# Renewing differences of keys at the changes of heads and of images, in a fused attention and non-local kernel

## The chip, the cores and the metric

The kernel runs on one core of a Trainium2 chip. The metric is the device time of one execution in microseconds (us); several executions are timed, and their median is given. One more execution is recorded by the hardware profiler; its page and its trace are what is read here. The engines are called PE (TensorE; PEld is its loading of weights), DVE (VectorE), ACT (ScalarE), POOL (GpSimd) and SP (SyncE, which here only issues transfers).

## What is computed

The input x is two images of 256 channels and 64 x 64 points, in float32. Layer 0 is full attention over the N = 4096 points of an image, with 8 heads of 32 channels, then a projection and a residual. Layer 1 is a non-local block (a second, smaller attention against pooled keys, with a normalization folded in), which follows it for each image. The part that the change touches belongs to layer 0:

```python
qkv = jnp.einsum('oc,bchw->bohw', w_qkv, x)
q, k, v = jnp.split(qkv, 3, axis=1)
...
scores = jnp.einsum('bhdi,bhdj->bhij', q, k) / jnp.sqrt(jnp.asarray(d, x.dtype))
attn = jax.nn.softmax(scores, axis=-1)
out = jnp.einsum('bhij,bhdj->bhdi', attn, v)
out = out.reshape(b, c, h, w)
return jnp.einsum('oc,bchw->bohw', w_proj, out) + x
```

## The kernel before

**Groups, blocks, steps.** The 8 heads of an image are worked in two groups of four, so that four heads of 32 channels fill 128 partitions. With two images there are four groups, n = 0 to 3 (the list QUAD, line 167, of pairs of image b and group qd). A group has 8 blocks of 512 queries (i = 0 to 7, NI = 8), and a block has 32 steps of 128 keys (j = 0 to 31, NJ = 32); this is the triple loop from line 576. Going from n = 0 to 1 and from 2 to 3 is a *change of heads* (the same image, the other four heads); going from 1 to 2 is the *change of images*: between the two groups stand the projection (project, line 629) and layer 1 (non_local, line 653) of the first image, and then the second image begins.

**A step.** PE makes scores of 128 keys against 512 queries of four heads, into two tiles of PSUM (score, line 439). ACT takes exp of each (line 598). PE weighs the values of the step before with their probabilities (weigh, line 472, its matmuls are line 476), and DVE or ACT takes the result from PSUM. The scores of a block stay in the same two tiles of PSUM from step to step: in place of writing new scores, a step *adds* to the old ones the product of the queries with the *difference* between its keys and those of the step before. The steps go through the keys in the order that line 437 gives: one 128-key part of each of the 8 chunks of 512 keys, then the next part of each. The differences lie in four tiles:

- kd (two differences, chunk 1 minus 0 and 3 minus 2), made anew for each group
- last_kd (two: 5 minus 4 and 7 minus 6), one tile for the whole program, line 223
- mid_kd (three: 2 minus 1, 4 minus 3, 6 minus 5), one tile, line 231
- turn_kd (from the last chunk's part to the next part of chunk 0), one tile, line 232

Within a block, score reads mid_kd at steps with j mod 8 = 2, 4, 6, last_kd at 5 (its first half) and 7 (its second half), and turn_kd at 8, 16 and 24.

**Maxima run ahead.** The softmax needs the greatest score of each query before its exponentials. These are worked out by a second pass over queries and keys, roughly one block ahead, in between the steps (maxima, line 382; product, line 290, with its matmuls at line 293). For two heads of four it uses differences too (pair, line 307): kd, and then last_kd. The maxima of a new group's first block run while the old group's last block still needs the old last_kd. For them before_all (line 275) makes the new group's two differences once more, in a tile first_kd, by two subtractions on POOL (line 227). The tile first_kd is a buffer of the pool xs under the tag "x", which has only one buffer: the loads of x for new queries, keys and values (make, line 171), first_kd, and the projection's weights (late_weights, line 97) take turns in it.

**Renewal.** renew (line 245) is called at the even steps: in blocks i > 0 while there is a next group, and in block 0 of groups 1 to 3. In a group's last block it makes the next group's mid_kd by POOL at steps 26, 28 and 30, when the last step that reads each third is over (between, line 234). In the next group's block 0, at steps 0 and 2, ACT copies the two halves of first_kd into last_kd (line 257), and at step 2 POOL makes turn_kd (rounds, line 238).

**Sums and buffers.** The sums of probabilities are made on two ways. Those of heads 0 and 1 are added by POOL at each step (line 509; the last one of a block is line 518). Those of heads 2 and 3 are kept for pairs of steps in tiles of 1024 KB (tag "two", five buffers) and added by accumulating transfers that POOL issues (line 515). When a block is over, normalize (line 520) adds the two accumulators by one more such transfer (line 524) and POOL adds the halves ("whole", line 528); then PE sums over the keys (line 536), ACT takes the result (line 544), the reciprocal goes by way of DRAM (lines 553 to 562, SP's queue), and POOL scales the block (line 573). For the last block of an image line 536 takes the sums as they are and DVE makes the reciprocal (line 547), in the midst of project. The tag "one" has six buffers for the probabilities of heads 0 and 1; project puts the loads x_res (line 635) into them.

**What sets the order.** [...]A scheduler lays the order down from the program's text, the dependences and its own costs: an operation may be placed earlier on its engine than the text has it. tc.issue_after only says that on that engine an instruction stands behind another; it is no wait. Waits on other engines and on buffers are put in by the framework.

Of the kernel before, what the change touches and what calls it, by code (L numbers as in the profile page):

```python
# [19 lines left out]
QUADS = HEADS // QH  # L20
# [5 lines left out]
NI = N // NB  # L26
NJ = N // P
# [8 lines left out]
def conv_attention(  # L36
# [13 lines left out]
    nc = tc.nc  # L50
# [17 lines left out]
    def scores(name):  # L68
        return ps_s.tile([P, 2, NB], F32, tag="s", name=name)
# [6 lines left out]
    def single(name):  # L76
        return probs.tile([P, 2, NB], F32, tag="one", name=name, bufs=ONES)

    def double(name):
        return probs.tile([P, 2, 2, NB], F32, tag="two", name=name, bufs=TWOS)  # L80
# [86 lines left out]
    QUAD = [(b, qd) for b in range(B) for qd in range(QUADS)]  # L167
# [55 lines left out]
    last_kd = const.tile([P, NI // 4, NB], F32, name="last_kd")  # L223

    def differences(n, c, to):
        two = k[n][:, bass.ts(c, 2 * NB)]
        nc.gpsimd.tensor_sub(to, two[:, NB:], two[:, :NB])
# [6 lines left out]
    def between(n, c):  # L234
        two = k[n][:, NB * (2 * c + 1) : NB * (2 * c + 3)]
        nc.gpsimd.tensor_sub(mid_kd[:, c, :], two[:, NB:], two[:, :NB])

    def rounds(n):
        nc.gpsimd.tensor_sub(
            turn_kd,  # L240
            k[n][:, P:NB].rearrange("p (a n) -> p a n", n=P),
            k[n][:, N - NB : N - P].rearrange("p (a n) -> p a n", n=P),
        )

    def renew(i, j, n):


        if (i, j) == (NI - 1, NJ - 6):
            between(n + 1, 0)
        elif (i, j) == (NI - 1, NJ - 4):  # L250
            between(n + 1, 1)
        elif (i, j) == (NI - 1, NJ - 2):
            between(n + 1, 2)
        elif (i, j) == (0, 2):
            rounds(n)
        if i == 0 and j in (0, 2):
            nc.scalar.copy(last_kd[:, j // 2, :], first_kd[n][:, j // 2, :])

# [1 line left out]
    first_kd = {}  # L262
# [159 lines left out]
    def attend(b, y):  # L422
# [73 lines left out]
        added = None  # L496
# [79 lines left out]
        for qd in range(QUADS):  # L576
            for i in range(NI):
                blk = Block(qd, i)
                items = during(blk.n, i)
                both = [None, None]  # L580
                for j in range(NJ):
                    if j % 2 == 0:
                        two = double(f"p_{blk.name}_{j}_1")
                    p = [single(f"p_{blk.name}_{j}_0"), two[:, j % 2]]
                    for pair in (1, 0):
                        if j == 0:
                            s = both[pair] = scores(f"s_{blk.name}_{j}_{pair}")
                            subtract(s, pair, blk)
                            advance(maxes)
                            score(s, pair, blk, j)  # L590
                        else:
                            s = both[pair]
                            score(s, pair, blk, j)
                            advance(maxes)
                        with ExitStack() as order:
                            if cut is not None:
                                order.enter_context(tc.issue_after(cut.ins))
                            nc.scalar.activation(p[pair], s, AF.Exp, scale=scale)  # L598
                    if waiting is not None:
                        weigh(*waiting)  # L600
                        if j == 0:
                            normal = normalize(waiting[0])
                    add(blk, j, p, two)
                    waiting = blk, j, p
                    if j in (1, 5) or j >= AFTER:
                        advance(normal)
                    if j % 2 == 0:
                        make_rows()
                        if i > 0 and blk.n + 1 < len(QUAD) or i == 0 and blk.n > 0:
                            with tc.issue_after(added.ins) if added else ExitStack():  # L610
                                renew(i, j, blk.n)
                        if i == NI // 2 and j in (12, 14) and blk.n + 1 < len(QUAD):
                            if j == 12:
                                kd[blk.n + 1] = qkv.tile(
                                    [P, NI // 4, NB], F32, tag="kd", name=f"kd_{blk.n + 1}"
                                )
                            with tc.issue_after(added.ins):
                                differences(blk.n + 1, j // 2 - 6, kd[blk.n + 1][:, j // 2 - 6, :])
                        if (i, j) == (NI - 1, 8) and blk.n + 1 < len(QUAD):
                            with tc.issue_after(added.ins):  # L620
                                before_all(blk.n + 1)
                    for item in items.get(j, ()):
                        if item[1] < len(QUAD):
                            advance(make(*item), 9)
# [290 lines left out]
```

## Time and profile before

| | |
|---|---|
| median of 3 executions | 3904.28 us (3903.01, 3904.28, 3907.87) |
| profiled execution, its own time | 3908.37 us |
| its span, first to last instruction | 3906.6 us, 69965 instructions |
| mean granted clock of PE | 0.997 |
| change of heads, n = 0 to 1 | copies at 903.5 and 910.1 us |
| change of images, n = 1 to 2 | copies at 1720.3 and 1726.9; projection's matmuls from 1734.85 |
| change of heads, n = 2 to 3 | copies at 2830.6 and 2837.1 us |

Times within the profile are counted from the span's start. A line of a group of instructions has the source line, the engine, the operation, the tiles (out<-in), shapes and the count; then durations in ns. In a line of the timeline stand the start, the time covered, the engine, the source line, the operation and the count, and in brackets how long the engine stood idle before it and what ended that. In a line of stretches stand the stretch, its length, each engine's busy time with the number of its instructions, PE's granted clock, the share of the transfer engines and GB/s.

The steps can be read off as the distance from the start of one weighing (line 476) to the next. Typical steps take 2.96 us; those in which keys, values or queries are made take more (6.85 us at step 30, 4.87 at 11, for example), and where a block's denominators are summed, 3.82. The last five distances of four blocks, and the first nine of the blocks after a change of heads beside an ordinary one, all in us:

```
end of an ordinary block (n = 1, i = 1)      2.96 2.96 6.85 3.13 2.96
end of an ordinary block (n = 3, i = 1)      2.96 2.96 3.29 3.13 2.96
end before a change of heads (n = 0, i = 7)  2.96 3.28 3.29 3.42 2.96
end before a change of heads (n = 2, i = 7)  2.96 3.28 3.29 3.42 2.96
first steps, ordinary (n = 1, i = 1)         2.96 2.96 2.96 2.96 2.96 2.96 2.96 3.82 2.96
first steps after a change (n = 1, i = 0)    2.96 2.96 2.96 2.96 2.96 4.14 2.96 5.09 2.96
first steps after a change (n = 3, i = 0)    2.96 2.96 2.96 4.74 2.96 5.13 2.96 4.34 2.96
```

### The profile page before, as it was taken

What the parts mean: (1) busy time and instruction counts of PE and PEld (TensorE: products, weight loads), DVE (VectorE), ACT (ScalarE), POOL (GpSimd) and SP (SyncE); (2) the same over time, 40 slices, a digit from 0 to 9 for tenths busy, and PEclk for the clock granted to TensorE, in tenths of its full rate; (3) what the DMA queues carried; (4) which work ended last, traced back from release to release, by engine and by line L of the source; (5) the groups of instructions that cost most, each with busy time, mean ns of one, the idle gap of its engine ahead of it and who ended that gap; (6) DMA issues with size and microseconds to landing.
All of it is one profiled execution on the core that took longest, in us unless ns stands there. A gap on an engine that the chain in (4) does not pass through costs nothing.

```text
span 3906.6 us, 69965 instructions
## 1 busy us (share of the span) xinstructions
PE 3864.0 (99%) x27452; PEld 1366.8 (35%) x27452; DVE 2900.7 (74%) x5449; ACT 2697.5 (69%) x3378; POOL 3091.5 (79%) x1957
## 2 busy tenths in 40 slices
PE   9999999999999999999999999999999999999998
PEld 4333333333333333333333333333333333332333
DVE  5888888788888888764458888888888888884444
ACT  5787777777777777751137777777778888887111
POOL 1888899899989999871448899998999999997043
PEclk9999999999999999999999999999999999999999
DMA  1778878778878788780018888887788888889100
GB/s 57 145 167 169 172 166 170 168 162 172 168 167 169 166 168 169 167 188 6 22 34 169 168 175 168 173 171 164 163 176 171 170 170 170 168 168 188 53 17 27
DMA packets 112300, 566.26 MB, mean 145 GB/s; under 512 B 20200, under 2 KB 22504, under 8 KB 50784
## 3 DMA queue, kind: packets, MB, share of 16 engines
q0 software_dynamic: 68832, 501.25, 63.5%
q1 hardware_dynamic: 42448, 59.74, 4.5%
q8 instruction: 215, 3.52, 0.3%
q14 instruction: 117, 0.96, 0.1%
q10 hardware_dynamic: 688, 0.79, 0.1%
HBM read 51.63 MB, written 8.88 MB: 15 GB/s over the span
## 4 chain that ended last, share of the span: by engine, by line
PE 96%; DVE 2%; DMA 1%; POOL 1%; issue 0%; ACT 0%; DVEq 0%; POOLq 0%; ACTq 0%; SPq 0%
PE s L452 28%; PE w L476 26%; PE ps L293 23%; PE y L771 6%; PE q L197 2%; PE k L197 2%; PE v L185 2%; PE proj L639 1%; PE g L696 1%; DVE r L785 1%; PE f L739 1%; PE f L805 1%; PE den L536 1%; DMA p<-p 1%; PE tp L680 0%; PE tp L676 0%
## 5 line engine op out<-in xcount | busy, mean ns | idle before, releaser
L509 POOL TENSOR_TENSOR p<-p,p 128x1024 f32<-128x1024 f32 x945 | 2364.4, 2502 | 281.4 <-ACT p L598 262.7
L598 ACT ACTIVATE p<-s 128x1024 f32<-128x1024 f32 x2048 | 2087.6, 1023 | 560.5 <-PE ps L293 495.1
L293 PE MATMUL ps<-k,q 32*128 32x512 f32 x6142 | 2020.6, 626 | 2.5 <-DVE r L785 1.3
L305 DVE TENSOR_REDUCE part<-ps 128x1 f32<-128x512 f32 x2046 | 1315.7, 686 | 566.8 <-PE ps L293 563.1
L476 PE MATMUL w<-p,v 128*32 128x512 f32 x8192 | 1091.0, 605 | 1.1 <-ACT p L598 1.1
L452 PE MATMUL s<-q,mid_kd 32*128 32x512 f32 x3072 | 771.2, 615 | 0.0
L320 DVE CUSTOM_DVE_ANT_0 ps<-ps,over 128x512 f32<-128x512 f32 x1025 | 706.2, 691 | 24.9 <-PE ps L293 10.5
L491 DVE TENSOR_TENSOR y<-y,w 128x512 f32<-128x512 f32 x961 | 659.1, 686 | 51.9 <-PE w L476 49.3
L293 PEld LDWEIGHTS ps<-k,q 32*128 32x128 f32 x6142 | 625.1, 183 | 25.6 <-DVE part L320 10.4
L313 ACT ACTIVATE over<-ps 128x512 f32<-128x512 f32 x961 | 569.3, 592 | 10.7 <-PE ps L293 7.9
L293 PE MATMUL ps<-kd,q 32*128 32x512 f32 x1056 | 525.9, 593 | 0.0
L452 PE MATMUL s<-q,last_kd 32*128 32x512 f32 x2048 | 508.5, 615 | 4.5 <-ACT p L598 4.5
L452 PE MATMUL s<-q,kd 32*128 32x512 f32 x2048 | 510.5, 616 | 0.4 <-ACT p L598 0.3
L293 PE MATMUL ps<-last_kd,q 32*128 32x512 f32 x904 | 445.1, 590 | 0.0
L476 PEld LDWEIGHTS w<-p,v 128*32 128x32 f32 x8192 | 161.6, 108 | 805.3 <-DVE part L305 775.2
L452 PEld LDWEIGHTS s<-q,mid_kd 32*128 32x128 f32 x3072 | 270.4, 183 | 443.5 <-ACT over L313 253.9
L515 POOL DMA_DIRECT2D p<-p x448 | 395.3, 882 | 27.3 <-ACT p L598 27.1
L452 PEld LDWEIGHTS s<-q,kd 32*128 32x128 f32 x2048 | 174.0, 184 | 299.8 <-ACT over L313 182.7
L452 PEld LDWEIGHTS s<-q,last_kd 32*128 32x128 f32 x2048 | 172.8, 183 | 284.9 <-ACT over L313 178.5
L771 PE MATMUL y<-p,kv 128*128 128x512 f32 x512 | 240.1, 608 | 6.4 <-DVE r L785 6.4
L820 ACT ACTIVATE p<-f 128x1024 f32<-128x1024 f32 x64 | 65.5, 1023 | 248.5 <-PE f L805 219.2
L767 POOL TENSOR_TENSOR sums<-sums,p 128x512 f32<-128x512 f32 x96 | 121.3, 1264 | 113.7 <-ACT p L820 109.9
(120 smaller groups left out, 2806.3 us busy)
## 6 DMA issues: line engine op xcount, KB each, us to landing
p<-p POOLq DMA_DIRECT2D x478, 1024.0 KB, 7.6
x_q<-in_x_dram SPq DMA_DIRECT2D x30, 512.0 KB
x_k<-in_x_dram SPq DMA_DIRECT2D x24, 512.0 KB
x_res<-in_x_dram SPq DMA_DIRECT2D x16, 512.0 KB
out_dram<-z SPq DMA_DIRECT2D x16, 512.0 KB
r<-flat SPq DMA_DIRECT2D x120, 64.0 KB
x<-in_x_dram SPq DMA_DIRECT2D x8, 512.0 KB
wqk_sb<-in_wqk_dram ACTq DMA_DIRECT2D x1, 512.0 KB
```

The source lines that it names most:

```text
L197: nc.tensor.matmul(pq, wqk_sb[:, c, qd, 0 if what == "q" else 1, :], xc[:, c, :], start=(c == 0), stop=(c == NC - 1),)
L293: nc.tensor.matmul(ps, q[n, i][bass.ts(h, D), bass.ts(g, P)], keys[bass.ts(h, D), :], start=True, stop=True,)
L305: reduced = nc.vector.tensor_reduce(part[:, g, h, j : j + 1], ps, AX.X, ALU.max)
L313: cut = nc.scalar.activation(over, ps, AF.Relu)
L320: reduced = nc.vector.tensor_tensor_reduce(out=ps, in0=ps, in1=over, scale=1.0, scalar=LEAST, op0=ALU.add, op1=ALU.max, accum_out=part[:, ...
L452: nc.tensor.matmul(s[:, t, :], kj[bass.ts(h, D), :], q[blk.n, blk.i][bass.ts(h, D), :], start=False, stop=True, skip_group_check=j > 0,)
L476: nc.tensor.matmul(w[bass.ts(h, D), :], v[blk.n][:, keys(j), h, :], p[h // 2][:, h % 2, :], start=True, stop=True,)
L491: nc.vector.tensor_add(blk.num, blk.num, w)
L509: added = nc.gpsimd.tensor_add(blk.sums[0], blk.sums[0], p[0])
L515: sent = nc.gpsimd.dma_start(out=blk.sums[n], in_=two, accum_op=ALU.add)
L598: nc.scalar.activation(p[pair], s, AF.Exp, scale=scale)
L771: nc.tensor.matmul(acc[i][o], wg[:, 2 * t + j, bass.ts(o, P)], p[:, j, :], **edge)
```

## The change

The function renew is written anew, and its caller calls it at every even step. In words:

- At a change of heads (the next group belongs to the same image) the two copies on ACT go. The first half of last_kd is filled by a transfer that SP issues at step 30 of the old group's last block, the second half by one issued at step 0 of the new group's first block; both read first_kd. The third difference of mid_kd moves from step 30 of the old block to step 0 of the new one. turn_kd moves from step 2 to step 4.
- At the change of images first_kd is no longer copied. All three differences of mid_kd, turn_kd and both halves of last_kd are made by POOL from the new group's keys, and all of them are written at step 0 of the new image's first block. (Before, mid_kd was written in the old image's last block, and last_kd came from first_kd.)

```diff
     def renew(i, j, n):
-        if (i, j) == (NI - 1, NJ - 6):
-            between(n + 1, 0)
-        elif (i, j) == (NI - 1, NJ - 4):
-            between(n + 1, 1)
-        elif (i, j) == (NI - 1, NJ - 2):
-            between(n + 1, 2)
-        elif (i, j) == (0, 2):
+        b, qd = QUAD[n]
+        if i == NI - 1 and qd < QUADS - 1:
+            if j in (NJ - 6, NJ - 4):
+                between(n + 1, (j - NJ + 6) // 2)
+            elif j == NJ - 2:
+                nc.sync.dma_start(out=last_kd[:, 0, :], in_=first_kd[n + 1][:, 0, :])
+        elif i == 0 and j == 0 and n > 0:
+            if qd > 0:
+                nc.sync.dma_start(out=last_kd[:, 1, :], in_=first_kd[n][:, 1, :])
+                between(n, 2)
+            else:
+                for c in range(NI // 2 - 1):
+                    between(n, c)
+                rounds(n)
+                for c in range(2):
+                    differences(n, NI // 4 + c, last_kd[:, c, :])
+        elif (i, j) == (0, 4) and qd > 0:
             rounds(n)
-        if i == 0 and j in (0, 2):
-            nc.scalar.copy(last_kd[:, j // 2, :], first_kd[n][:, j // 2, :])
...
                     if j % 2 == 0:
                         make_rows()
-                        if i > 0 and blk.n + 1 < len(QUAD) or i == 0 and blk.n > 0:
-                            with tc.issue_after(added.ins) if added else ExitStack():
-                                renew(i, j, blk.n)
+                        with tc.issue_after(added.ins) if added else ExitStack():
+                            renew(i, j, blk.n)
```

The built programs differ as follows, engine by engine. PE and DVE execute the same instructions in the same order. ACT loses six copies. SP gains four transfers: both of each change of heads stand behind the transfers of the sixth block's denominators and ahead of the next load of x; at the change of images g's two weights move ahead of the load x_res 6. POOL has two more subtractions. At a change of heads mid_kd's third difference stands behind the old block's last addition (line 518), and turn_kd two additions later than before. At the change of images the scheduler has placed all six subtractions in the old image's last block, between the additions of steps 23 and 31: turn_kd ahead of step 24's, mid_kd ahead of 26's, 28's and 30's, last_kd ahead of 29's and 31's; before, only the three of mid_kd stood there, behind 26's, 28's and 30's.

## The prediction

> **What bounds the kernel now.** I read the busy shares and the chain of waits first, then every instruction that touches the tiles of the change, then the timeline around the three changes of group.
>
> ```profile
> PE 3864.0 (99%) x27452; PEld 1366.8 (35%) x27452; DVE 2900.7 (74%) x5449; ACT 2697.5 (69%) x3378; POOL 3091.5 (79%) x1957
> ...
> PE 96%; DVE 2%; DMA 1%; POOL 1%; issue 0%; ACT 0%; DVEq 0%; POOLq 0%; ACTq 0%; SPq 0%
> ```
>
> TensorE carries 96% of the chain. So only what makes PE wait or run slower counts. In the timeline of line 476 (one weighing for each step of 128 keys) nearly every step takes 2.96 us; a change gains where a step at a change of group is longer than the same step elsewhere.
>
> ```profile
> L257 ACT COPY last_kd<-first_kd x6: 612/613/614, 903.5 to 2837.1; 128x512 f32<-128x512 f32 x6
> ...
> L236 POOL TENSOR_TENSOR mid_kd<-k x12: 1264/1268/1287, 17.3 to 2842.2; 128x512 f32<-128x512 f32 x12
> ...
> L239 POOL TENSOR_TENSOR turn_kd<-k x4: 996/1154/1301, 53.3 to 2856.8; 128x384 f32<-128x384 f32 x4
> ```
>
> These are the operations that the change removes or moves: six copies on ACT of 0.61 us, subtractions on POOL of 1.27 us (512 columns) and some 1.15 us (384). The dear place is the change of images:
>
> ```profile
> 1726.89 0.61 ACT L257 COPY last_kd<-first_kd 128x512 f32<-128x512 f32 x1
> ...
> 1727.57 0.40 SPq L103 DMA_DIRECT2D weights<-in_wproj_dram  x1
> ...
> 1728.97 1.06 PE L476 MATMUL w<-p,v 128*32 128x512 f32 x8 [1.14 <-ACT p L598]
> 1734.85 6.43 PE L639 MATMUL proj<-y,weights 128*128 128x512 f32 x9 [4.81 <-DMA weights<-in_wproj_dram]
> ...
> 1732.00:1740.00 8.00, 5.15 (x7) 2.36 (x8) 0.00 (x0) 0.00 (x0) 5.55 (x4) 0.57 1.01 258
> ```
>
> The projection's weights go into the buffer that first_kd holds, so their load is issued only when the second copy is over (1727.51), and PE stands 4.81 us for it. Then it runs at a granted clock of 0.57 (the last line, 1732 to 1740 us). At the two changes of heads something else waits:
>
> ```profile
> 924.76 0.87 POOL L524 DMA_DIRECT2D p<-p  x1 [2.78 <-DMA p<-p]
> ...
> 931.69 1.02 ACT L598 ACTIVATE p<-s 128x1024 f32<-128x1024 f32 x1 [1.90 <-DMA p<-p]
> ...
> 939.28 1.02 ACT L598 ACTIVATE p<-s 128x1024 f32<-128x1024 f32 x1 [2.38 <-POOL whole L528]
> ...
> 2853.92 0.87 POOL L524 DMA_DIRECT2D p<-p  x1 [4.95 <-DMA p<-p]
> ...
> 2861.55 1.02 ACT L598 ACTIVATE p<-s 128x1024 f32<-128x1024 f32 x1 [2.88 <-DMA p<-p]
> ...
> 2868.39 1.02 ACT L598 ACTIVATE p<-s 128x1024 f32<-128x1024 f32 x1 [1.63 <-POOL whole L528]
> ```
>
> POOL, which has not been idle for over 0.15 us at a time since 842 us, stands before line 524 until the old block's last accumulating transfer (line 515, issued 916.42) has landed; everything behind it is late, and the exponentials find no free buffer. By the steps: 4.14 for 2.96 and 5.09 for 3.82 us (2.45 lost) after the first change of heads; 4.74, 5.13 for 2.96 and 4.34 for 3.82 (4.47 lost) after the second.
>
> **What the skill says.** "TensorE: Matmul & The Clock Gate", What's actually happening: PE falls to half clock after an idle window of some 3.4 us of a free-running grid. The trace agrees: its clock record has half speed for 6.83 us from 1732.71, 2.7 us after the last weighing ended at 1730.03. "DMA: Bandwidth & Descriptors", Issuing engines are not separate DMA queues: all transfers share 16 engines. The trace agrees, and shows more: the load of x issued by SP at 910.74 moved its first packet 4.7 us later, when the accumulation issued at 909.57 was nearly through. The same page, Anatomy of one DMA, gives 2.0 us plus bytes over 436 GB/s: 4.4 us for 1024 KB, where the page of this profile has 7.6, so I don't use it.
>
> **The change, part by part.**
> *Copies off ACT.* The closing steps of a block without K and V to make are 2.96, 2.96, 3.29, 3.13 us (blocks of the last group); before a change of heads they are 2.96, 3.28, 3.29, 3.42. So two copies cost 0.32 + 0.29 = 0.61 us of PE, not 1.23. At the change of images the second stands straight before the last exponential, on which PE waits: 0.32 + 0.61 = 0.9 us. On a change of heads the 0.61 gains nothing by itself: what follows waits for POOL's queue, whose times do not depend on ACT there.
>
> *Change of images.* In the built program's order the weights now wait for PE's last read of first_kd, which in the trace is at 1710.6, not for a copy. Four issues of 0.40 to 1.44 us put them on the rings by about 1716, 14 us before PE wants them. The wait of 4.81 us goes. With it the half clock: the seven starts from 1734.85 to 1740.25 take 5.40 us where full speed takes 7 x 0.43 = 3.0, 2.4 lost. What is late next: "later" holds only for the text of the program. In the built order the scheduler puts all renewals before the old image's last addition: POOL has turn_kd (1.15 us) moved ahead and two subtractions into last_kd (2 x 1.27) added, and it is in arrears there (gaps of 0.08 us). So the last transfer of sums (line 515, 1733.09) is issued 1.15 + 1.27 = 2.4 us later, at 1735.5; the last addition (line 518, over at 1736.34) is over 3.7 us later, at 1740.0; the loads of x_res, which take over buffers that those additions free, are issued from some 1722 to 1740 instead of 1732.3 to 1736.4. PE, starting to project at about 1729.3, needs the denominators after 32 matmuls x 0.43 = 13.8 us, at 1743.1, and the transfer (8.5 to 9 us with two loads beside it; it took 10.0 before) lands at about 1744.3. The first four matmuls need older sums and take about 0.8; I charge 0.4 us. The order of loads of x_res and g's weights in SP's queue also changes; x_res was never late by more than 0.8 us in all, nothing. Sum: 0.9 + 4.8 + 2.4 - 0.4 = **7.7 us**, bounds 4 (half clock stays, sums are late by 1 more) and 8.2.
>
> *Changes of heads.* Two transfers of 256 KB each replace the copies. No row shows an SBUF copy by SP's queue. From above, a quarter of an accumulation of 1024 KB (some 5.2 us of all 16 engines in the packet records): 1.3 us of the rings; from below, half a 512 KB load of x (some 1.6): 0.8. I take 0.8. The first is issued when the last step's scores have been read (903.4, 2830.5), moves between two accumulations and costs nothing; the rings are empty from 908 to 910.5. Its reader comes 7 steps later, 20 us. The second is issued at 909.9 beside the accumulation of 909.57. Behind both in SP's queue stand x's next load (used at step 11, over 30 us on) and the transfers of denominators (first needed at 942): room enough. The third difference (mid_kd) moves behind the last accumulation's issue and the addition of line 518: that transfer is issued 1.27 us earlier. mid_kd is then ready at 919.4, for use at step 6 (929). turn_kd moves behind two additions: ready at some 932.6 instead of 929.0, for step 8 (936.2); 3.6 us of room.
> The landing comes earlier by at most 1.27 us at the first change, minus what the rings lose: x's load of 512 KB lay before that transfer and may still, and 256 KB come on top. Bounds -0.3 and 1.2; I take **0.6**. At the second change the loads of x, gw and ww (1 MB, issued 2837.8 to 2842) pushed that transfer to a landing at 2853.38, 10.0 us after its issue; if the new order keeps them behind it, 3.5 us are to be had, of which they give some back before line 524's transfer; if not, 1. Bounds 0.5 and 3; I take **1.7**. POOL's queue sets all later times up to "whole", so these are the gains of PE.
>
> Sum: 7.7 + 0.6 + 1.7 = 10.0 us. The profiled execution took 3908.37 us, 1.8 over its span of 3906.6: it would take 3898.4. It is 4.1 us above the median of the three runs; part may be a second half-clock stretch at 2022.84 (6.83 us, some 3 lost), which depends on where the grid falls and may come or go. I subtract from the median: 3904.28 - 10.0 = **3894.3 us**. A difference of 0.2% (7.8 us) is about what a measurement of this kernel can tell from no change.
>
> **The rivals.**
> *A, forecast, 0.62:* 3891 to 3896.4.
> *B, the changes of heads are cleared whole, 0.10:* all 2.45 + 4.47 + 2 x 0.61 = 8.1 us there, with 7.7: 3888.5. For it: POOL's gap of 4.95 us at 2853.92 is pure waiting. Against: POOL does the same subtractions before "whole" as before.
> *C, the wait for weights becomes a wait for sums, 0.24:* POOL's 3.7 us more in arrears, and half clock at another place; the change of images gives 4 and the heads 0.5: 3899.8, no change that can be told. For it: POOL's gaps of 0.08 us. Against: denominators stood finished 8 us before use (landed 1743.1, used 1751.1).
> *D, slower, 0.04:* the copies hold the rings ahead of the old block's last accumulations. Each us that such a landing is late passes through line 524 to the exponentials. From 16 us in both changes together it outweighs 7.7 and 8 more: about 3913. It needs a copy of 256 KB to take 8 us instead of 0.8 to 1.3.
> That the renewals between images don't come later is not a rival but counted above.
>
> **How the numbers follow.** Faster by over 0.2%: A and B, 0.72; within: C, 0.24; slower: D, 0.04. The range covers A and C, with B and D (0.14) left out: 3890 to 3901.
>
> **What would show it.** Line 639's first matmul starts within 0.3 us of the last weighing, no half clock near it, weights issued at about 1711 to 1716. Line 536 at the change of images waits under 1 us. Closing steps before a change of heads are 2.96, 2.96, 3.29, 3.13. The landing before line 524 comes 0 to 1.2 and 1 to 3.5 us earlier against POOL's own work. Wrong if PE still stands over 2 us at line 639 or 536, or if exponentials wait longer for line 524 than 1.9 and 2.9 us in sum with the rest.

## The result, and the profile after

| | before | after |
|---|---|---|
| median (22 runs each, taken together) | 3904.86 us | 3899.11 us |
| lowest and highest | 3903.01, 3912.77 | 3896.64, 3906.32 |
| profiled execution: own time, span | 3908.37, 3906.6 | 3898.32, 3896.5 |
| its mean granted clock of PE | 0.997 | 0.999 |

The ratio is 0.9985, with a 95% interval of 0.9978 to 0.9991: 5.8 us less, between 3.5 and 8.6. The forecast was 10.0 less (0.9974). The two profiled executions differ by 10.1 us, but a single execution of this kernel scatters by some us, as will be seen.

In the changed kernel the lines behind renew stand lower: 293 is now 301, 476 is 484, 515 is 523, 518 is 526, 524 is 532, 528 is 536, 536 is 544, 598 is 606, 639 is 646. The page's busy shares and its chain of waits are almost the same; the change is too small for them.

```profile
PE 3859.2 (99%) x27452; PEld 1362.3 (35%) x27452; DVE 2899.8 (74%) x5449; ACT 2694.4 (69%) x3372; POOL 3092.7 (79%) x1959
...
PE 95%; DVE 2%; DMA 1%; POOL 1%; issue 0%; ACT 0%; DVEq 0%; POOLq 0%; ACTq 0%
```

**The change of images.** The timeline of SP's queue, of PE, and the stretch from 1732 to 1740 us, all of the changed kernel:

```profile
1712.27 0.40 SPq L103 DMA_DIRECT2D weights<-in_wproj_dram  x1
```

```profile
1729.07 1.07 PE L484 MATMUL w<-p,v 128*32 128x512 f32 x8 [0.63 <-ACT p L606]
1730.07 14.00 PE L646 MATMUL proj<-y,weights 128*128 128x512 f32 x32
1744.00 1.06 PE L544 MATMUL den<-p,ones 128*32 128x512 f32 x8
1745.67 2.77 PE L544 MATMUL den<-p,ones 128*32 128x512 f32 x12 [0.60 <-DMA p<-p]
```

```profile
1732.00:1740.00 8.00, 8.00 (x20) 3.50 (x19) 2.45 (x2) 0.00 (x0) 8.00 (x7) 1.00 1.00 248
```

The denominators of the kernel before, on PE's timeline:

```profile
1751.08 3.64 PE L536 MATMUL den<-p,ones 128*32 128x512 f32 x20
```

The weights are issued 15 us earlier than before, and the projection starts straight behind the last weighing, with no bracket of idle time. The granted clock of the stretch is 1.00 where it was 0.57. One small wait has come: after eight matmuls of the denominators PE stands 0.60 us until the last transfer of sums has landed.

**The changes of heads.** The two transfers and x's next load in SP's queue at the first change; then POOL's issues of the last accumulation (line 523) and of the adding transfer (line 532), and its addition of the halves, whole (line 536); then ACT's exponentials with their waits at both changes, all of the changed kernel:

```profile
903.01 0.53 SPq L253 DMA_DIRECT2D last_kd<-first_kd  x1
909.27 0.49 SPq L256 DMA_DIRECT2D last_kd<-first_kd  x1
911.62 0.40 SPq L88 DMA_DIRECT2D x_q<-in_x_dram  x1
```

```profile
914.74 0.86 POOL L523 DMA_DIRECT2D p<-p  x1
...
925.42 0.87 POOL L532 DMA_DIRECT2D p<-p  x1 [3.88 <-DMA p<-p]
...
937.38 2.65 POOL L536 TENSOR_TENSOR whole<-p 128x1024 f32<-128x1024 f32 x1
```

```profile
924.97 1.02 ACT L606 ACTIVATE p<-s 128x1024 f32<-128x1024 f32 x1 [2.10 <-DMA p<-p]
...
932.36 1.02 ACT L606 ACTIVATE p<-s 128x1024 f32<-128x1024 f32 x1 [2.19 <-DMA p<-p]
...
940.06 1.03 ACT L606 ACTIVATE p<-s 128x1024 f32<-128x1024 f32 x1 [2.49 <-POOL whole L536]
...
2839.71 1.02 ACT L606 ACTIVATE p<-s 128x1024 f32<-128x1024 f32 x1 [2.38 <-DMA p<-p]
...
2853.28 1.02 ACT L606 ACTIVATE p<-s 128x1024 f32<-128x1024 f32 x1 [2.46 <-PE w L484]
```

In the kernel before, x's next load, the last accumulation and whole stood at the first change so:

```profile
910.74 0.40 SPq L88 DMA_DIRECT2D x_q<-in_x_dram  x1
```

```profile
916.42 0.85 POOL L515 DMA_DIRECT2D p<-p  x1
...
936.61 2.64 POOL L528 TENSOR_TENSOR whole<-p 128x1024 f32<-128x1024 f32 x1
```

At the first change POOL's wait before the adding transfer has grown from 2.78 to 3.88 us, and an exponential now waits 2.10 us for the last accumulation itself, and another 2.19 us for the adding transfer. The waits at both places have changed their form; whether PE gained can only be told from a sum over blocks.

**A measure that reads the changes of heads in one number.** The closing steps, the exponentials and the waits shift time between them, so I sum the old group's last block and the new group's first, from weighing to weighing. In the same count (from the first weighing of the old group's last block) stand below the issue and landing of the old block's last accumulation, the landing of the adding transfer, and the end of whole on POOL. All in us:

| change | kernel | last accumulation | adding transfer lands | whole ends | two blocks |
|---|---|---|---|---|---|
| 0 to 1 | before | 98.85 to 106.64 | 114.03 | 121.67 | 202.87 |
| 0 to 1 | after | 97.61 to 107.75 | 115.15 | 122.90 | 204.10 |
| 2 to 3 | before | 98.74 to 108.72 | 116.81 | 123.70 | 201.34 |
| 2 to 3 | after | 97.48 to 106.91 | 115.62 | 122.04 | 199.68 |

The two blocks take whole's end plus 81.20 us at the first change and plus 77.64 at the second, in both kernels. So one time decides: when whole is over. The first change loses 1.23 us, the second gains 1.66. Over all fourteen traces of this study the same two figures hold to 0.03 us at 21 of the 28 changes of heads; of the other seven, five have a stretch at half clock behind the change, and two are those of the kernel with two renewals left out.

The whole difference of the two profiled executions: change of images 7.2 (388.74 us before and 381.52 after, from the first weighing of the old image's last block to the first matmul of line 301, before it 293, with which the next image begins; then another 0.9, where a half-clock stretch lasted 3.41 us in place of 6.83), changes of heads -1.23 and +1.66, ahead of the first weighing 0.4, from the last block on 1.3, all other blocks -0.2: 10.0 us. Of these, 7.2 - 1.23 + 1.66 = 7.6 us lie where the change touches the program.

### The profile page after: what moved, and what is told of

The parts are those of the page before. It is cut to its first block, busy times and chain, and to the rows that moved or that the text cites. A ratio compares the mean times of both kernels' runs of the same rounds, so it can differ in the third digit from the quotient of the medians.

```text
span 3896.5 us, 69971 instructions
## 1 busy us (share of the span) xinstructions
PE 3859.2 (99%) x27452; PEld 1362.3 (35%) x27452; DVE 2899.8 (74%) x5449; ACT 2694.4 (69%) x3372; POOL 3092.7 (79%) x1959
## 4 chain that ended last, share of the span: by engine, by line
PE 95%; DVE 2%; DMA 1%; POOL 1%; issue 0%; ACT 0%; DVEq 0%; POOLq 0%; ACTq 0%
PE s L460 28%; PE w L484 26%; PE ps L301 23%; PE y L778 6%; PE q L197 2%; PE k L197 2%; PE v L185 2%; PE g L703 1%; DVE r L792 1%; PE f L746 1%; PE f L812 1%; PE proj L646 1%; DMA p<-p 1%; PE den L544 1%; PE tp L687 0%; PE tp L683 0%
```

## The experiments

Theory 1 after the result: the change of images brings all of it, and the changes of heads give and take in about equal parts. Theory 2: the heads bring a good part. Three kernels take one half of the change each or another way to the same end, and one is the kernel before once more. Each is shown as a diff against the changed kernel, unless another is named, or in words; the diffs are shortened, and (i, j) ahead of a colon stands for the condition under which the call is made.

**Images alone.** At the changes of heads, renew as before; at the change of images as changed.

```diff
-elif i == NI - 1 and j == NJ - 2: nc.sync.dma_start(out=last_kd[:, 0, :], ...)
-(0, 0): nc.sync.dma_start(out=last_kd[:, 1, :], ...); between(n, 2)     (0, 4): rounds(n)
+j = NJ - 2: between(n + 1, 2)     (0, 2): rounds(n)
+(0, 0), (0, 2): nc.scalar.copy(last_kd[:, j // 2, :], first_kd[n][:, j // 2, :])
```

> The change of images as in the changed kernel, the two changes of heads as in the kernel before. Theory 1 (the image change earns all, the head changes next to nothing): from the last block of group 1 to the first weighing of group 2 some 387.5 us instead of 395.6, the head changes' blocks as before (98.7 + 104.1 and 98.7 + 102.6 us), time 0.9980 of before. Theory 2 (the head changes earn a good part of the 5.8 us): 0.9990 or more.

Measured: 3900.2 against 3906.58 us, ratio 0.9983 [0.9975, 0.9991]. As much as the whole change gave (0.9985), within the intervals. Two blocks: 202.91 us, as before, and 202.08, with 3.41 us at half clock in it.

**Heads alone.** The other half: the changed text at the changes of heads, the old one at the change of images.

> The two changes of heads as in the changed kernel, the change of images as in the kernel before (copies on ACT, PE's wait for the weights stays). Theory 1: the transfers lengthen the accumulations that are under way; the blocks at the first change of heads take some 204.1 us instead of 202.9, at the second 199.7 instead of 201.3; time 1.0000 of before within 0.0006. Theory 2 (as predicted, 2.3 us earned here, or more): 0.9994 or less, both pairs of blocks shorter.

Measured: 3907.16 against 3906.58 us, ratio 1.0001 [0.9992, 1.0009]. Two blocks: 204.20 and 199.72 us, the changed kernel's own numbers to 0.1. The wait for the weights is back (4.72 us), and the 6.83 us at half clock with it. Theory 2 falls by its two blocks, which had to be shorter at both changes; the interval alone would still hold its 0.9994.

**Another release of the weights.** Heads as before. At the change of images only the two copies of first_kd are replaced; mid_kd and turn_kd stay where they were. (The diff is against the kernel before.)

```diff
-nc.scalar.copy(last_kd[:, j // 2, :], first_kd[n][:, j // 2, :])
+differences(n, NI // 4 + j // 2, last_kd[:, j // 2, :])
```

> As the kernel before, only that at the change of images last_kd is made by POOL from the keys instead of being copied from first_kd, at the places in the text where the copies stood. mid_kd and turn_kd stay. Theory (the freed buffer is the whole gain): weights issued at about 1711 us, no wait at the projection, no half clock there, and the last transfer of sums lands about 1.2 us earlier than in the changed kernel, so PE's wait of 0.6 us ahead of line 536's work goes too: group 1's last block to group 2's first weighing in 387 us or less, time 0.9979. Rival (the renewals' new places in POOL's order are part of the gain): 388.5 or more.

Measured: 3900.82 against 3906.58 us, ratio 0.9980 [0.9973, 0.9988]. Its stretch from the last block's first weighing to the next image's first is 386.25 us (before 395.59, after 387.47), and PE's timeline has no wait in it:

```profile
1727.70 14.00 PE L645 MATMUL proj<-y,weights 128*128 128x512 f32 x32
1741.63 3.64 PE L543 MATMUL den<-p,ones 128*32 128x512 f32 x20
```

The twenty matmuls of the denominators run through. So what pays is that nothing reads first_kd late. Up to the first matmul of the next image this stretch is 0.76 us shorter than the changed kernel's, of which the wait is 0.60: that is what the new places of mid_kd and turn_kd cost. The other 0.46 us lie behind that point, where the changed kernel has 3.41 us at half clock and this one has none.

**The kernel before, again.**

> The kernel before once more, for a second profile and for the scatter of the comparison. Expected 1.0000 within 0.0006. If half clock after the change of images (2022.84 us in the first profile) depends on where a free-running grid falls, its place or length differs here; the half clock at the projection (PE idle 4.8 us) is there again, with 1.5 to 3.4 us lost; the distances at the changes of heads repeat within 0.2 us.

Measured: 3907.39 against 3906.58 us, ratio 1.0001 [0.9993, 1.001]. Its trace shows what scatters: the wait for the weights was 5.63 us in place of 4.81, the half-clock stretch near 2024 us lasted 3.41 in place of 6.83, there was another of 3.41 at 3625, and from the last block on it took 379.0 us in place of 376.2. Profiles of single executions can't settle 2 us of the whole; sums over two blocks can, since they repeat to 0.2 us (202.74 and 201.20 here, 202.87 and 201.34 in the first).

The next four ask what the heads' part is made of. All have the changed kernel's change of images. Theory 1: POOL's new order (third difference of mid_kd behind the last addition) gives the gain, the transfers take it back on the rings (the 16 transfer engines with their queues).

**ACT's copies, POOL's new order.**

```diff
-nc.sync.dma_start(out=last_kd[:, c, :], in_=first_kd[...][:, c, :])     (c = 0 at step 30, c = 1 at step 0)
+nc.scalar.copy(last_kd[:, j // 2, :], first_kd[n][:, j // 2, :])     (at steps 0 and 2)
```

> As the changed kernel at the change of images; at the changes of heads the two copies stay on ACT (at steps 0 and 2, as before), while POOL's order is that of the changed kernel (third of mid_kd behind the old block's last addition, turn_kd two additions later). Sums of the last and the first nine-step stretch, read as whole blocks: before 98.74 and 104.14 us at the first change, 98.73 and 102.61 at the second; changed kernel 98.11, 106.00 and 98.11, 101.57. Theory 1 (POOL's new order gives the gain, the two transfers take it back on the rings): the first block after the change falls to about 103 at the first change and to 101 or less at the second, the last block stays at 98.7; heads give 2 to 4 us in sum, 3896 to 3898 us when before is 3906. Theory 2 (POOL's new order is what costs, since line 518 and turn_kd are late): the first change stays at 106 and the whole is 3901.

Measured: 3900.11 against 3905.84 us, ratio 0.9984 [0.9978, 0.9991]; two blocks 202.60 and 201.68. The last accumulation is issued 1.2 us earlier, at 97.65 and 97.48, but lands only 0.4 earlier at the first change (106.25) and 0.2 later at the second (108.94). The new order alone gives next to nothing: both theories missed, the first most of all.

**Transfers, POOL's old order.**

```diff
-(0, 0): between(n, 2)     (0, 4): rounds(n)
+j = NJ - 2: between(n + 1, 2)     (0, 2): rounds(n)
```

> As the changed kernel at the change of images; at the changes of heads the two transfers by SP take the place of ACT's copies, but POOL's order is that of before (mid_kd's third at step 30, turn_kd at step 2). Theory 1 (transfers cost, POOL's order gains): closing block 98.1, first blocks 106 or more at the first change and 102.6 or more at the second, that is, 1 to 4 us lost at the heads; 3901 to 3904 us when before is 3906. Theory 2 (POOL's order costs, transfers are free): first blocks 104.1 and 102.6, the heads give 1.2 from the closing steps, 3899 us.

Measured: 3898.23 against 3905.84 us, ratio 0.9981 [0.9974, 0.9988]; two blocks 204.23 and 199.69, again the changed kernel's numbers. The last accumulation lands at 108.03 and 107.05. So the transfers make both the loss of the first change and the gain of the second, which neither theory had: I had expected them to cost at both.

**The second transfer on POOL's queue.** It is issued behind the third difference, that is, behind the old block's last accumulation.

```diff
-nc.sync.dma_start(out=last_kd[:, 1, :], in_=first_kd[n][:, 1, :])
 between(n, 2)
+nc.gpsimd.dma_start(out=last_kd[:, 1, :], in_=first_kd[n][:, 1, :])
```

> As the changed kernel, but the second half of last_kd is filled by a transfer that POOL issues behind the third subtraction of mid_kd, so on the queue that carries the accumulations, behind the old block's last one. Theory 1 (what costs is that this copy, issued beside the accumulations, shares the rings with them, and frees x's buffer too early or too late): the accumulation of step 28 lands as before (8.4 us after its issue in place of 10.2 at the second change), x's next load is issued only after the copy and so behind the old block's last accumulation, first blocks 103 and 101 us; 3896 to 3898 us when before is 3906. Rival (the copy on POOL's queue delays the transfer of line 524 behind it, and POOL pays some 0.9 us to issue it): first blocks 106 and 103 or more, 3901 us or more.

Measured: 3898.94 against 3905.84 us, ratio 0.9982 [0.9973, 0.9990]; two blocks 201.58 and 201.37. Now x's load is issued only when that transfer has landed (924.21 us at the first change), behind the last accumulation, which lands at 105.24 and 105.34, the earliest of all up to here. At the first change this reaches PE: 2.5 us less than the changed kernel. At the second it does not: three loads (x's, and the two weights that layer 1 needs for g and behind it, called g's weights, 1 MB in all) are issued within 1.1 us of the adding transfer, which then takes 9.9 us (8.1 at the first change), and behind the wait PE falls to half clock for 3.41 us. There the two blocks exceed whole's end by 80.95 in place of 77.64: the measure holds only while whole ends the last long wait; here no exponential waits for whole, and the last long wait is one of 3.56 us for the adding transfer.

**Copies on DVE, POOL's new order.**

```diff
+nc.vector.tensor_copy(last_kd[:, j // 2, :], first_kd[n][:, j // 2, :])     (at steps 0 and 2)
```

> As the kernel with ACT's copies and POOL's new order, but with the two copies on DVE in place of ACT. Theory 1 (copies off the rings and off ACT take nothing from PE): closing blocks 98.1 and first blocks as low as with ACT's copies, 103 and 101 us, so about 1.2 us less than that kernel in sum; 3895 to 3897 us when before is 3906. Rival (DVE takes weighed sums out of PSUM[...]): first blocks 104 to 106, 3899 us or more.

Measured: 3898.93 against 3905.84 us, ratio 0.9981 [0.9973, 0.9988]; two blocks 202.71 and 200.12. The copies took 0.95 to 2.26 us, and the old block's last steps grew (3.97 and 5.04 us where 2.96 and 3.13 stand in the changed kernel); the old block is 101.04, not 98.11 as theory 1 had it. In exchange the first block is only 101.67 and 99.28. At the first change whole ends at 121.50, as with ACT's copies (121.42), and the sum is the same to 0.1. That is the measure at work: a delay of PE ahead of whole is given back behind it. The rival's slower additions did not come: beside the copies POOL's additions took 2.36 to 2.65 us, with ACT's copies 2.36 to 2.66.

The theory after these: what counts is which loads lie on the rings ahead of, or beside, the last accumulation and the adding transfer. Four more kernels test it. In all four ACT copies the second half only behind the exponential of step 4, which holds x's load back.

**Late release alone.** POOL's old order, both copies on ACT, at steps 0 and 4.

```diff
+with tc.issue_after(latest["exp"].ins):
+    nc.scalar.copy(last_kd[:, j // 4, :], first_kd[n][:, j // 4, :])     (at steps 0 and 4)
```

> As the changed kernel at the change of images. At the changes of heads as the kernel before (ACT copies both halves, POOL's order is that of before), but the copies stand two and four steps later on ACT: behind the exponentials of steps 0 and 4 of the new block. So x's next load can only be issued some 14 us later, behind the old block's last accumulation; g's two weights still go ahead of it at the second change. Sums of the last and first block over the two changes, before: 202.88 and 201.34 us. Theory 1 (the place of x's load against the old block's last accumulation is what decides; the transfers of copies matter through that): that accumulation lands within 8 us of its issue, the old block's end is 98.1 (the copies no longer stand before PE there) and the sums are about 201 and 199.5, so 3 to 4 us less in all; 3895 to 3897 us when before is 3906. Theory 2 (POOL's arrears alone set the sum, whatever lies on the rings): 202.5 and 201, 3898 us.

Measured: 3900.88 against 3906.0 us, ratio 0.9987 [0.9980, 0.9993]; two blocks 203.72 and 201.05. The last accumulation lands 7.5 and 8.4 us after its issue (at the second change g's weights are ahead), near the forecast; the time is not, and theory 1 missed. PE, no longer slowed earlier, comes to the adding transfer in one wait of 1.9 us, at each change, and falls to half clock for 3.41 us. Two blocks exceed whole's end by 82.37 and 78.97 here in place of 81.20 and 77.64: 1.2 and 1.3 us, which I put down to the half clock. Without it the sums would be, by an estimate from the measure, 202.5 and 199.7, a gain of 0.3 and 1.6.

**Candidate.** The release of the weights by the subtractions of "another release"; at the heads the first half by SP's transfer at step 30, the second by ACT behind step 4's exponential, POOL's new order.

> The best of both: at the change of images mid_kd and turn_kd as before, and last_kd by two subtractions on POOL at steps 0 and 2 (no copy of first_kd); at the changes of heads the first half by SP's transfer at step 30, the second by ACT behind the exponential of step 4, POOL's order as in the changed kernel. Image stretch (first weighing of the last block to the first of the next image) 386.3 us against 387.5 changed and 395.6 before. Theory 1 (x's load behind the old block's last accumulation): closing block 98.1, sums over the changes of heads about 201 and 199 against 202.88 and 201.34 before, 204.11 and 199.68 changed; 3893 to 3895 us when before is 3906. Theory 2 (only POOL's arrears): 202.3 and 200.8, 3896 us.

Measured: 3896.16 against 3906.0 us, ratio 0.9977 [0.9968, 0.9985]; two blocks 201.54 and 201.51. The first is nearer to theory 1, the second is above both, and the time is theory 2's. At the first change POOL's timeline has the last accumulation and the adding transfer so:

```profile
914.66 0.87 POOL L528 DMA_DIRECT2D p<-p  x1
...
922.71 0.87 POOL L537 DMA_DIRECT2D p<-p  x1 [1.24 <-ACT p L611]
```

POOL's wait is 1.24 us where it was 2.78 before and 3.88 after. (The bracket names ACT, but the adding transfer is issued 0.54 us behind the landing of the last accumulation, as in the kernel before and in the changed one.) Late release, with POOL's old order, had whole end at 121.35 at this change, the candidate at 120.35: with x's load held back, an issue 1.19 us earlier brought a landing 1.15 us earlier, where with x's load ahead (ACT's copies, before) 1.20 brought 0.39. The two kernels also differ in what fills the first half of last_kd. At the second change g's weights are issued 1.5 and 1.0 us ahead of the last accumulation; it takes 9.8 us, POOL waits 3.53, and PE falls to half clock once more. PE's timeline there, and the stretch behind it:

```profile
2850.91 0.70 PE L465 MATMUL s<-q,last_kd 32*128 32x512 f32 x2 [1.93 <-ACT p L611]
```

```profile
2851.70:2855.10 3.40, 3.40 (x17) 1.05 (x16) 1.38 (x2) 1.67 (x3) 3.40 (x3) 0.50 0.94 193
```

**Candidate with two renewals left out.**

Against the candidate; the kernel leaves out part of the computation, and only prices POOL's work.

```diff
-(0, 0): between(n, 2)
-(0, 4): rounds(n)
```

> As the candidate, but at the two changes of heads the third difference of mid_kd and turn_kd are left out, so that the new group goes on with those of the old group (part of the computation is changed). It takes 1.27 + 1.0 us from POOL between the old block's last addition and the line that adds the halves (whole), at each change, and nothing from any other engine. Theory POOL's arrears (what is left of PE's waits, some 3 us at each change, is POOL's work up to that line): each sum falls by 1.5 to 2.3 us against the candidate, 3889 to 3891. Theory chain of transfers (the last accumulation, then the adding transfer of line 524, then the halves, set the exponentials): under 0.7 us each, and exponentials still wait for the adding transfer.

Measured: 3896.29 against 3906.0 us, ratio 0.9976 [0.9966, 0.9986]; two blocks 201.00 and 199.70. POOL has 2.3 us less to do at each change, whole ends 1.0 and 1.2 us earlier, and PE gains 0.5 at the first change. At the second it gains 1.8, of which about 1.2 is the half clock that did not come this time (the wait of PE ahead of it was 1.92 us, as long as in the candidate). The two blocks exceed whole's end by 81.61 and 78.22, so whole alone no longer sets the sum: at the second change no exponential waits for it, and the last long wait is one of 3.16 us for the adding transfer; at the first one still waits 0.68 us for whole. POOL's work is worth about a quarter of its length; that the chain of two transfers holds the rest is inferred, not shown.

**Candidate with g's weights later.** Against the candidate; on SP's queue they stand behind the next but one load of x.

```diff
+with tc.issue_after(loads[f"x_q_{QUADS * b + QUADS - 1}_3"].ins):
     nc.sync.dma_start(out=gw_sb, ...)
     nc.sync.dma_start(out=ww_sb, ...)
```

> The candidate, with one thing more: on SP's queue the loads of g's two weights (256 KB each, which the second image's layer 1 uses some 700 us later) stand behind the next but one load of x, and so not in the second change of heads. The first change, the image change and every instruction of the other engines are the candidate's. In the candidate the old block's last accumulation of the second change landed 9.8 us after its issue with g's weights issued 1.5 us ahead of it, where the first change, with nothing ahead, had 7.5; the two blocks summed to 201.51 us. Theory 1 (each load that lies ahead of that accumulation costs PE its time on the rings): it lands within 8 us, the wait of 1.9 us for the accumulation before it goes too, and the sum falls to 199.2 to 200.2; the whole to 3894 to 3896 us when before is 3906. Theory 2 (POOL's arrears and the chain of two transfers take it back): 201 us or more, no change against the candidate.

Measured: 3895.69 against 3907.53 us, ratio 0.9968 [0.9956, 0.9981], the lowest ratio of the study, though its interval overlaps the candidate's; two blocks 201.59 and 198.21, the second lower than forecast. POOL's timeline at the second change:

```profile
2831.24 0.86 POOL L530 DMA_DIRECT2D p<-p  x1
...
2839.44 0.87 POOL L539 DMA_DIRECT2D p<-p  x1 [1.40 <-ACT over L328]
```

The last accumulation takes 7.7 us (9.8 in the candidate), whole ends 2.1 us earlier, and PE gains 3.3: those 2.1, and 1.2 from the half clock that is gone. One order in one queue did the 2.1; the half clock may or may not have gone with it (with two renewals left out it was gone too, with g's weights ahead). This settles the theory for the second change; the first change's 201.6 repeats the candidate's.

## Why the prediction was right or wrong

**Closing steps: right.** 2.96, 2.96, 3.29, 3.13 before both changes of heads, 0.62 us less in the block (98.11 for 98.73). That this gains nothing by itself was right too: the sum follows whole's end to 0.1 us.

**Change of images: right, 7.2 for 7.7.** The projection's first matmul comes 5.66 us earlier from the block's start (0.9 + 4.8 = 5.7 in the sum), the denominators' first 7.95 earlier, so the half clock was 2.3 (2.4 in the sum). The wait for sums cost 0.77 in all (0.4 in the sum): the transfer was issued at 1735.5 as worked out, and took 10.1 us in place of 8.5 to 9. The Trainium skill ("TensorE: Matmul & The Clock Gate", What's actually happening) lets PE fall to half clock after an idle window; that the 6.83 us at half clock went with the wait of 4.81 us agrees with it. Rival C's price, a second wait of several us, did not come.

**Changes of heads: 2.3 forecast, 0.4 measured; this step failed.** The second change was right in size, 1.66 for 1.7, and in its cause as one of the two cases named: the loads of x, gw and ww were kept behind the last accumulation, which landed 1.8 us earlier against the block (1 to 3.5 forecast). But it was the slow second transfer, not POOL's new order, that held first_kd's buffer until x's load could be issued at 2839.86, as the two kernels with one half each show.
The first change failed in "that transfer is issued 1.27 us earlier" taken as an earlier landing. It was issued 1.24 us earlier, and landed 1.11 later (forecast: 0 to 1.2 earlier; bounds of PE's gain -0.3 to 1.2, measured -1.23). From 911 to 923 us the rings were busy without a pause, in both kernels: one accumulation, x's load, the last accumulation. On these busy rings an earlier issue moved little (ACT's copies with POOL's new order: 1.2 us at issue, 0.4 at landing), and what was put ahead moved the landing. The second copy took 0.75 us of all 16 engines (from the packet records; I had 0.8), between 909 and 911.5, where the rings had been free, but at the end of that gap: the accumulation behind it ended 0.45 us later, and x's load, issued only when the copy had landed (93.2 before, 94.5 after, counted from the block's start), still went ahead of the last accumulation. The price of the copy was right; "the landing comes earlier" was wrong, since I read the chain from POOL's issue and not from the queue on the rings. The other 0.66 us of the 1.11 I can't assign to one packet. With that came a sign of being wrong that the prediction named: exponentials wait 2.10 and 2.19 us for the two transfers, where one of 1.90 stood before.

**Copy beside an accumulation: mis-sized at the second change.** There the second transfer moved from 2831 to 2838 us, on some 4 of 16 engines, 1.5 us of all engines in sum, and the accumulation beside it took 10.2 us in place of 8.4; an exponential waits 2.38 us for it. That is above both bounds of the prediction, 0.8 and 1.3. By the measure above this wait cost nothing of its own, but the 0.8 was not general.

**The sum: too large by 4.2 us against the medians.** 1.8 of that is the first change of heads, 0.5 the change of images. The parts measured inside one trace give 7.2 + 0.4 = 7.6, within the interval of 3.5 to 8.6 around 5.8. That the changed kernel's profiled execution took 3898.32 us, where 3898.4 was forecast for it, is luck: the 2.4 us that the parts fall short came from elsewhere (0.9 + 0.4 + 1.3 - 0.2). Whether the remaining 1.8 us are chance in the medians or half-clock stretches that come elsewhere in other executions stays open: stretches at 2014 to 2026, 2854, 3532 and 3625 us came and went between profiled executions of like kernels, each worth some 0.5 to 3 us.

**Rivals.** The time fell between A and C. The prediction gave 0.72 to a gain of over 0.2%; the measured 0.15% is the outcome that it gave 0.24, C's "no change that can be told". But C's reason is not what happened: the change of images kept 7.2, not 4. D's mechanism, copies ahead of the last accumulation, was real at the first change, at a fourteenth of the 16 us that it needed. B's 8.1 us at the heads were partly to be had after all, by orders of loads and not by the copies: the kernel with the lowest ratio has 202.87 - 201.59 = 1.3 and 201.34 - 198.21 = 3.1.

## What to carry to other kernels

When waits move around without a sum that changes, find the one late event that everything behind it is measured from (here the end of whole), and express each variant as a shift of that event. Before counting on an earlier issue of a transfer, look whether the rings are busy up to its start: if so, what lies ahead of it can count for more than when it is issued, and the place of an unhurried load in its queue (weights first used 805 us after their issue in the candidate) can be worth more than the copy that one set out to remove: here 2.1 us at one change against 0.62 for two copies. A buffer that is freed late is a way to hold a load back, on purpose or not.

## What the runs showed that I had not expected

- A wait of PE of 1.93 us, inside one step, was followed by 3.41 us at a granted clock of 0.50 in the candidate; a wait of 1.92 us in the kernel with two renewals left out was not. With images alone a wait of 1.51 us was followed by such a stretch, with another release of the weights one of 1.51 us at the same place was not; PE's lines of these last two stand below. The Trainium skill ("TensorE: Matmul & The Clock Gate", What's actually happening) speaks of an idle window of some 3.4 us; here less was enough, and the measurement decides. The same holds for the half clock at the projection, which the prediction read as agreeing: it came 2.7 us after the last weighing. So the length of a wait does not tell by itself whether half clock follows, and each kernel has one trace, so how often it follows is not known. Where it did at a change of heads, two blocks exceeded whole's end by 1.0 to 1.3 us more than elsewhere (images alone, late release, the candidate).
- An SBUF copy of 256 KB by SP's queue, issued 0.3 us behind an accumulation of 1024 KB, shared the engines with it for 7 us at the second change, while at the first, issued 0.2 us behind one, it moved ahead of it in 2.5 us. x's load in the same place waited for the accumulation's end (4.7 us) in the kernel before. The order in which the packets of two queues take turns was not the same in like cases, and no run here shows the rule.
- The same accumulation of 1024 KB took 7.1 us with no load and no copy beside it (candidate, first change, next to last of the block) and 11.5 with loads of 1 MB ahead of it (ACT's copies with POOL's new order, second change).

PE's timeline of the two waits of 1.51 us, images alone first (half clock from 2854.28 us on), then another release of the weights (none):

```profile
2852.64 0.70 PE L459 MATMUL s<-q,last_kd 32*128 32x512 f32 x2 [1.51 <-ACT p L605]
```

```profile
2851.73 0.70 PE L459 MATMUL s<-q,last_kd 32*128 32x512 f32 x2 [1.51 <-ACT p L605]
```
